# A mixture-of-experts block on one core: the last sequence's attention and shared experts move behind the routed tiles, and tokens are put in order in steps over two sequences

## The chip, the cores and the metric

The kernel runs on one core of a Trainium2 chip. The metric is the device time of one execution in microseconds (us). TensorE is called PE below, VectorE is DVE, ScalarE is ACT, GpSimd is POOL and SyncE is SP.

## The reference

There are 16 sequences of 512 tokens with 256 features. With `xn = layernorm(x)`, the output is `x + attention(xn) + ffn(xn)`, all in float32:

```
q, k = elu(xn@Wq+bq)+1, elu(xn@Wk+bk)+1 ;  v = xn@Wv+bv          # 16 heads of 16
attention = ((q @ (k^T v)) / max(q . sum(k), 1e-6)) @ Wo + bo    # linear, not causal, per sequence
shared    = swiglu(xn @ w_in^T) @ w_out^T                        # hidden 512
h         = swiglu(xn @ w1^T)                                    # hidden 512
group     = argmax of 2 group logits ; 2 best of its 4 experts, with weights p
routed    = sum over the 2 chosen experts e of  p_e * h @ w2[e]^T
```

A token therefore has one of 12 pairs of experts (6 in each group).

## The kernel before

**Dense part.** A loop over the 16 sequences `b` runs, for each: `front(b+1)` one sequence ahead (keys and logits into `pk`, queries into `pq`, the feature map, the routing in `route`), `summarize` (`pxk`, keys times inputs), `hidden_rows` (`phr`, the routed experts' hidden rows `h`, four tiles of 128 tokens, stored to a DRAM table `h_d`), `key_sum` and `attend` (`pks`, then normalized queries written to DRAM and read back turned), `hidden` (`phs`, the shared experts' hidden features `hs_all`), `mix` (`pvk`, DVE's `vk`, then `pm`, then ACT's copy `kvo`), and `gather` (`po`, for each of four token tiles four products with `wout_sb` and two with `kvo`, added to `res` by DVE and stored to `h_d` beside `h`). So one row of `h_d` holds 512 hidden values, 256 values of everything but the routed part, and two weights.

**Order.** Once all tokens are routed, `order` sorts them by pair. It counts (`pc`), computes each token's slot, and builds for eight groups `g` of eight token tiles the one-hot factors `lo` and `hi` on DVE, whose products `pi` on PE give, for each of 75 tiles of 128 slots, which token sits where. It is called at the start of the last sequence (`b = 15`), between `front` and `summarize`.

**Routed part.** Pairs of tiles (`class Tiles`): `rows` gathers 128 rows of `h_d` by an indirect DMA of POOL into one of four buffers that the dense part no longer uses; `turn` transposes the hidden values (12 ACT copies to `hb`, 7 DVE transposes to `hT`); `sums` multiplies with the pair's two experts (`py`), scales and adds the row's other 256 values on DVE (`y`), and scatters whole rows to `out` by an indirect DMA of POOL. 67 tiles are always run; more stand in a conditional block (`rest`, with `tc.If(n > i)`), which is skipped with these inputs. The first three pairs are gathered twice: before `gather(15)`, to turn the hidden values early, and after it, when the rest of the row has been stored.

**What sets the order.** Each engine runs its own instructions in the order in which the program lists them. A scheduler makes that list when the kernel is built; `tc.keep_in_program_order` pins an instruction in it, and `tc.issue_after(x)` keeps one behind another. An instruction that waits holds up all that is behind it on its engine. PSUM has six buffers named `mm` in a ring (all products but `po`, `py`'s included) and two named `py` (used by `po` and `pi`).

Lines that are spoken of below, with the numbers of the profile: L242 the DVE transpose that places `xnT` and `qT`, L424 `phr`, L443 `phs`, L482 `pvk`, L489 and L494 `vk`, L499 `pm`, L534 `po`, L535 its addition, L545 and L546 `pc`, L598 to L612 `lo` and `hi`, L614 `pi`, L654 `rows`, L673 to L686 `turn`, L703 `py`, L711 and L714 `y`, L717 the scatter, L783 the load of the count `n` into registers, L801 the conditional.

Of the kernel before, what the change touches and what calls it, by code (L numbers as in the profile page):

```python
# [15 lines left out]
P = 128  # L16
# [5 lines left out]
def block_kernel(  # L22
# [60 lines left out]
    wp = ctx.enter_context(tc.tile_pool(name="weights", bufs=1))  # L83
    xp = ctx.enter_context(tc.tile_pool(name="x", bufs=2))
    keep = ctx.enter_context(tc.tile_pool(name="keep", bufs=1))
# [11 lines left out]
    out_rows = out.rearrange("b s d -> (b s) d")  # L97

    def load_x(b, pieces=1):
        xt = xp.tile([P, NT, D], FP, tag="x", name=f"x_{b}")  # L100
        n = NT // pieces
        for i in range(pieces):
            nc.sync.dma_start(
                out=xt[:, ts(i, n), :], in_=x[b, ts(i, n * P), :].rearrange("(t p) d -> p t d", p=P)
            )
        return xt
# [109 lines left out]
    for c in range(NP):  # L216
        nc.gpsimd.memset(steps[:, c : c + 1], float(spots[c] - (spots[c - 1] if c else 0)))

    kk_all, qq_all, xn_all = (keep.tile([P, 2, NT, D], FP, name=f"{n}_all") for n in ("kk", "qq", "xn"))
    hs_all = keep.tile([P, KH, S], FP, name="hs_all")

# [192 lines left out]

    def hidden_rows(b, xnT):

        for t in range(NT):
            halves = []  # L420
            for half in range(2):
                ph = ps_mm.tile([P, HID], FP, tag="mm", name=f"phr_{b}_{t}_{half}")
                for k in range(KD):
                    nc.tensor.matmul(  # L424
                        ph, lhsT=xnT[:, k, ts(t, P)], rhs=w1_sb[:, k, ts(half, HID)],
                        start=(k == 0), stop=(k == KD - 1),
                    )
                halves.append(ph)
            sa = work.tile([P, HID], FP, tag="sa", name=f"sa_hr_{b}_{t}")
            nc.scalar.activation(sa, halves[0], AF.Silu)  # L430
            hr = work.tile([P, HID], FP, tag="hr", name=f"hr_{b}_{t}", bufs=3)
            nc.vector.tensor_tensor(hr, halves[1], sa, ALU.mult)  # L432
            nc.sync.dma_start(out=h_d[ts(b * NT + t, P), 0:HID], in_=hr)

    def hidden(b, xnT):

        h = hs_all
        for f in range(KH):
            halves = []
            for half in range(2):  # L440
                ph = ps_mm.tile([P, S], FP, tag="mm", name=f"phs_{b}_{f}_{half}")
                for k in range(KD):
                    nc.tensor.matmul(  # L443
                        ph, lhsT=win_sb[:, k, ts(half * KH + f, P)], rhs=xnT[:, k, :],
                        start=(k == 0), stop=(k == KD - 1),
                    )
                halves.append(ph)
            sa = work.tile([P, S], FP, tag="sa", name=f"sa_hs_{b}_{f}")
            nc.scalar.activation(sa, halves[0], AF.Silu)  # L449
            nc.vector.tensor_tensor(h[:, f, :], halves[1], sa, ALU.mult)  # L450
        return h

# [72 lines left out]

    def gather(b, res, qT, kvo, hs):

        taken = []
        for t in range(NT):
            po = ps_y.tile([P, D], FP, tag="py", name=f"po_{b}_{t}")  # L530
            parts = [(hs[:, f, ts(t, P)], wout_sb[:, f, :]) for f in range(KH)]
            parts += [(qT[:, c, ts(t, P)], kvo[:, c, :]) for c in range(KD)]
            for i, (a, w) in enumerate(parts):
                nc.tensor.matmul(po, lhsT=a, rhs=w, start=(i == 0), stop=(i == len(parts) - 1))  # L534
            taken.append(nc.vector.tensor_tensor(res[:, t, 0:D], po, res[:, t, 0:D], ALU.add))  # L535
            nc.sync.dma_start(out=h_d[ts(b * NT + t, P), HID:ROW], in_=res[:, t, :])
        return taken

    def order():
# [4 lines left out]
        pc = ps_mm.tile([P, 2 * NP], FP, tag="mm", name="pc")  # L544
        nc.tensor.matmul(pc[:, 0:NP], lhsT=before, rhs=total, start=True, stop=True)  # L545
        nc.tensor.matmul(pc[:, NP:], lhsT=ones, rhs=total, start=True, stop=True)  # L546
# [43 lines left out]
        where = keep.tile([P, TR], I32)  # L590
        nc.vector.tensor_copy(where, of)


        pi = ps_y.tile([P, 2 * TILES], FP, tag="py", name="pi")
        for g in range(TT // TG):
            row_of, tile_of = (place_of[:, i, ts(g, TG)].unsqueeze(2) for i in range(2))
            lo = xp.tile([P, TG, P], BF, tag="x", name=f"lo_{g}")
            nc.vector.tensor_tensor(  # L598
# [7 lines left out]
            )  # L606
            hi = work.tile([P, TG, 2, TILES], BF, tag="blocks", name=f"hi_{g}")
            nc.vector.tensor_tensor(
                hi[:, :, 0, :], at_tile,
                number[:, ts(g, TG)].unsqueeze(2).to_broadcast([P, TG, TILES]), ALU.mult,  # L610
            )
            nc.vector.tensor_scalar(hi[:, :, 1, :], at_tile, row, None, ALU.mult)  # L612
            for t in range(TG):
                nc.tensor.matmul(  # L614
                    pi, lhsT=lo[:, t, :], rhs=hi[:, t].rearrange("p i n -> p (i n)"),
                    start=(g + t == 0), stop=(g * TG + t == TT - 1),
                )
        pis = keep.tile([P, 2, TILES], FP)
# [15 lines left out]
        nc.vector.scalar_tensor_tensor(goal, tok, float(-P), free, ALU.add, ALU.add)  # L634
        return source, goal, where, filled

    regs = []

    rows_of = [a.rearrange("p a b c -> p (a b c)") for a in (kk_all, qq_all, xn_all)]
    rows_of.append(hs_all.rearrange("p a b -> p (a b)"))  # L640

    class Tiles:
# [16 lines left out]

        def turn(self, after=None):  # L660

# [3 lines left out]

            n, W = self.n, HID // NQ
            self.hT = work.tile([P, KH, 2 * P], FP, tag="xnT", name=f"hT_{self.tiles[0]}")
            to = self.hT.rearrange("p c (n a j) -> p n c a j", n=2, a=NQ)[:, 0:n]
            near = 1
            there = work.tile([P, NQ - near, 2, W], FP, tag="blocks", name=f"hb_{self.tiles[0]}")  # L670
            for a in range(near, NQ):
                for q in range(NQ):
                    nc.scalar.copy(  # L673
                        there[ts(q, Q), a - near, 0:n, :], self.hg[ts(a, Q), 0:n, ts(q, W)]
                    )
            wait = (lambda: tc.issue_after(after.ins)) if after else nullcontext
            for a in range(near):
                for q in range(NQ):
                    with wait():
                        nc.vector.transpose(  # L680
# [3 lines left out]
            for a in range(near, NQ):  # L684
                with wait():
                    self.turned = nc.vector.transpose(  # L686
                        to[:, :, :, a, :],
                        there[:, a - near, 0:n, :].rearrange("p n (c i) -> p n c i", i=Q),
                    )
            return self  # L690

        def sums(self, after=None):

            for j, i in enumerate(self.tiles):
# [14 lines left out]
                y = work.tile([P, D], FP, tag="y", name=f"y_{i}", bufs=4)  # L709
                with tc.issue_after(after.ins) if after else nullcontext():  # L710
                    nc.vector.scalar_tensor_tensor(  # L711
                        y, py[:, 0, :], base[:, D : D + 1], base[:, 0:D], ALU.mult, ALU.add
                    )
                nc.vector.scalar_tensor_tensor(  # L714
# [25 lines left out]
    for b in range(B):  # L740
        xn, xnT, _ = normed.pop(b)
        res, qq, kk = fronts.pop(b)
        if b + 1 < B:
            fronts[b + 1] = front(b + 1, normed[b + 1][1])
        else:

            nc.sync.dma_start(
                out=h_d[ts(b, S), HID:ROW].rearrange("(t p) h -> p t h", p=P), in_=res
            )
            *lists, filled = order()  # L750
            tiles = [Tiles(list(range(i, min(i + 2, SURE))), *lists) for i in range(0, SURE, 2)]
# [6 lines left out]
        if b + 3 < B:  # L758
            xs[b + 3] = load_x(b + 3)
        hidden_rows(b, xnT)  # L760
        ksb, (qT, turned) = sums, queries.pop(b)
        turned()
        if b + 1 < B:
            sums = key_sum(b + 1, fronts[b + 1][2])
            queries[b + 1] = attend(b + 1, fronts[b + 1][1], sums)
        hs = hidden(b, xnT)
        kvo = mix(b, xk, ksb)
        if b + 2 < B:
            normed[b + 2][2]()
        if b + 1 == B:  # L770
            for w in tiles[:AHEAD]:
                w.rows()
        taken = gather(b, res, qT, kvo, hs)
        if b + 1 == B:

            tiles[0].turn(taken[-2])
            for w in tiles[1:AHEAD]:
                w.turn(taken[-1])

# [7 lines left out]

    tiles[AHEAD].rows()
    for w in tiles[:AHEAD]:
        w.rows()  # L790
    for g, w in enumerate(tiles):
        if 0 < g < len(tiles) - AHEAD:
            tiles[g + AHEAD].rows()
        if 0 < g < len(tiles) - AHEAD + 1:
            tiles[g + AHEAD - 1].turn()

        w.sums(tiles[AHEAD - 1].turned if g == 0 else None)

# [12 lines left out]

    rest(SURE)


# [30 lines left out]
```

## Time and profile before

| what | value |
|---|---|
| three runs | 1079.85, 1085.42, 1088.38 us; median 1085.42 us |
| the profiled execution's own time | 1076.49 us |
| its span in the profile | 1074.8 us |
| PE busy | 1052.6 us (98%), 3404 matmuls |
| DVE busy | 661.1 us (62%) |
| ACT busy | 375.9 us (35%) |
| POOL busy | 244.9 us (23%) |
| DMA | 116.02 MB, mean 108 GB/s |

The profile is of one execution. "Busy" is the share of the span in which an engine had an instruction running; a matmul's end is modelled, so a busy PE is not a PE at its peak. A view "in order of time" gives the start, the length, the engine, the source line, the operation, the output and inputs, how many, and in brackets how long the engine had stood idle before and who released it.

### The profile page before, as it was taken

What the parts mean: (1) busy time and instruction counts of PE and PEld (TensorE: products, weight loads), DVE (VectorE), ACT (ScalarE), POOL (GpSimd) and SP (SyncE); (2) the same over time, 40 slices, a digit from 0 to 9 for tenths busy, and PEclk for the clock granted to TensorE, in tenths of its full rate; (3) what the DMA queues carried; (4) which work ended last, traced back from release to release, by engine and by line L of the source; (5) the groups of instructions that cost most, each with busy time, mean ns of one, the idle gap of its engine ahead of it and who ended that gap; (6) DMA issues with size and microseconds to landing.
All of it is one profiled execution on the core that took longest, in us unless ns stands there. A gap on an engine that the chain in (4) does not pass through costs nothing.

```text
span 1074.8 us, 11307 instructions
## 1 busy us (share of the span) xinstructions
PE 1052.6 (98%) x3404; PEld 624.7 (58%) x3404; DVE 661.1 (62%) x1744; ACT 375.9 (35%) x703; POOL 244.9 (23%) x313
## 2 busy tenths in 40 slices
PE   7999999999999999999999999999999999999996
PEld 6474848475756666575748484757566444444442
DVE  7947476565647474747465565646386576666663
ACT  3413132222222231313131322212113686667771
POOL 6102011020202020201011010202002665555552
PEclk9999999999999999999999999999999999999999
DMA  7243342424424242423231313131212654555440
GB/s 231 98 118 118 79 137 59 137 75 122 115 86 139 66 134 69 138 59 106 71 103 55 118 40 118 40 98 60 64 55 95 207 173 147 153 155 151 149 152 29
DMA packets 129054, 116.02 MB, mean 108 GB/s; under 512 B 72109, under 2 KB 113597, under 8 KB 128736
## 3 DMA queue, kind: packets, MB, share of 16 engines
q1 hardware_dynamic: 119120, 77.16, 24.0%
q0 software_dynamic: 9456, 37.59, 11.4%
q8 instruction: 29, 0.48, 0.2%
q10 hardware_dynamic: 416, 0.52, 0.1%
q14 instruction: 33, 0.27, 0.1%
HBM read 65.36 MB, written 50.27 MB: 108 GB/s over the span
## 4 chain that ended last, share of the span: by engine, by line
PE 91%; DVE 4%; DMA 2%; issue 1%; ACT 1%; POOL 1%; SPq 0%; POOLq 0%; ACTq 0%; DVEq 0%
PE phs L443 20%; PE py L703 20%; PE phr L424 19%; PE po L534 15%; PE pk L312 5%; PE pxk L469 5%; PE pq L323 5%; PE pm L499 1%; PE pvk L482 1%; DMA kk_all<-h_d,source 1%; PE pks L459 1%; ACT hb L673 1%; DMA xn_all<-h_d,source 0%; DMA x<-in_x 0%; DVE qm L300 0%
## 5 line engine op out<-in xcount | busy, mean ns | idle before, releaser
L703 PE MATMUL py<-w_sb,hT 128*128 x536 | 230.5, 592 | 2.0 <-DVE hT L686 2.0
L443 PE MATMUL phs<-xnT,win_sb 128*128 128x512 f32 x512 | 223.7, 593 | 0.0
L424 PE MATMUL phr<-w_sb,xnT 128*128 128x512 f32 x512 | 222.8, 592 | 0.0
L703 PEld LDWEIGHTS py<-w_sb,hT 128*128 128x128 f32 x536 | 101.7, 190 | 130.5 <-issue 129.3
L424 PEld LDWEIGHTS phr<-w_sb,xnT 128*128 128x128 f32 x512 | 97.1, 190 | 114.7 <-issue 105.9
L443 PEld LDWEIGHTS phs<-xnT,win_sb 128*128 128x128 f32 x512 | 96.6, 190 | 113.5 <-issue 110.0
L292 POOL TENSOR_TENSOR res<-x,bo_sb 128x1024 f32<-128x1024 f32 x16 | 38.9, 2432 | 435.0 <-DMA h_d<-res 324.0
L534 PE MATMUL po<-wout_sb,hs_all 128*128 128x256 f32 x512 | 123.6, 379 | 0.0
L535 DVE TENSOR_TENSOR res<-po,res 128x256 f32<-128x256 f32 x64 | 27.2, 424 | 131.8 <-PE po L534 131.8
L534 PEld LDWEIGHTS po<-wout_sb,hs_all 128*128 128x128 f32 x512 | 96.1, 190 | 12.4
L450 DVE TENSOR_TENSOR hs_all<-phs,sa_hs 128x512 f32<-128x512 f32 x64 | 43.4, 679 | 90.2 <-PE phs L443 84.9
L449 ACT ACTIVATE sa_hs<-phs 128x512 f32<-128x512 f32 x64 | 38.2, 597 | 157.8 <-PE phs L443 152.4
L717 POOL DMA_INDIRECT out<-y,goal x67 | 67.7, 1010 | 76.2 <-DVE y L714 65.5
L301 ACT ACTIVATE km<-km 128x1024 f32<-128x1024 f32 x16 | 16.9, 1058 | 178.0 <-DVE km L300 172.9
L432 DVE TENSOR_TENSOR hr<-phr,sa_hr 128x512 f32<-128x512 f32 x64 | 43.7, 684 | 55.0 <-PE phr L424 32.1
L430 ACT ACTIVATE sa_hr<-phr 128x512 f32<-128x512 f32 x64 | 38.0, 597 | 99.0 <-PE phr L424 93.1
L534 PE MATMUL po<-kvo,qT 128*128 128x256 f32 x256 | 67.0, 384 | 0.0
L312 PE MATMUL pk<-wkr_sb,xnT 128*128 128x266 f32 x256 | 61.0, 391 | 1.7 <-DVE xnT L242 1.7
L469 PE MATMUL pxk<-kk_all,xn_all 128*128 128x256 f32 x256 | 57.9, 379 | 0.0
L323 PE MATMUL pq<-wq_sb,xnT 128*128 128x256 f32 x256 | 57.8, 379 | 0.0
L456 POOL TENSOR_TENSOR k<-kk_all 128x512 f32<-128x512 f32 x16 | 27.6, 1723 | 125.4 <-DVE sm L358 119.3
L312 PEld LDWEIGHTS pk<-wkr_sb,xnT 128*128 128x128 f32 x256 | 48.9, 192 | 10.8 <-DVE xnT L242 2.1
(148 smaller groups left out, 1261.0 us busy)
## 6 DMA issues: line engine op xcount, KB each, us to landing
h_d<-hr SPq DMA_DIRECT2D x64, 256.0 KB, 2.6
h_d<-res SPq DMA_DIRECT2D x64, 129.0 KB, 2.0
q_d<-qq_all SPq DMA_DIRECT2D x16, 512.0 KB, 2.8
qb<-q_d SPq DMA_DIRECT2D x64, 128.0 KB, 2.6
w_sb<-in_w SPq DMA_DIRECT2D x64, 128.0 KB, 3.5
x<-in_x SPq DMA_DIRECT2D x15, 512.0 KB, 4.3
xn_d<-xn_all SPq DMA_DIRECT2D x14, 512.0 KB, 3.0
xb<-xn_d SPq DMA_DIRECT2D x56, 128.0 KB, 3.2
```

The source lines that it names most:

```text
L292: nc.gpsimd.tensor_tensor(res[:, :, 0:D], xs.pop(b), bo_sb.unsqueeze(1).to_broadcast([P, NT, D]), ALU.add)
L312: nc.tensor.matmul(pk, lhsT=xnT[:, k, ts(t, P)], rhs=wkr_sb[:, k, :], start=(k == 0), stop=(k == KD - 1),)
L323: nc.tensor.matmul(pq[:, t, :], lhsT=xnT[:, k, ts(t2 + t, P)], rhs=wq_sb[:, k, :], start=(k == 0), stop=(k == KD - 1),)
L424: nc.tensor.matmul(ph, lhsT=xnT[:, k, ts(t, P)], rhs=w1_sb[:, k, ts(half, HID)], start=(k == 0), stop=(k == KD - 1),)
L432: nc.vector.tensor_tensor(hr, halves[1], sa, ALU.mult)
L443: nc.tensor.matmul(ph, lhsT=win_sb[:, k, ts(half * KH + f, P)], rhs=xnT[:, k, :], start=(k == 0), stop=(k == KD - 1),)
L449: nc.scalar.activation(sa, halves[0], AF.Silu)
L450: nc.vector.tensor_tensor(h[:, f, :], halves[1], sa, ALU.mult)
L469: nc.tensor.matmul(pxk[:, c, :], lhsT=xn[:, t, ts(c, P)], rhs=kk[:, t, :], start=(t == 0), stop=(t == NT - 1),)
L534: nc.tensor.matmul(po, lhsT=a, rhs=w, start=(i == 0), stop=(i == len(parts) - 1))
L703: nc.tensor.matmul(py.rearrange("p j d -> p (j d)"), lhsT=self.hT[:, f, ts(j, P)], rhs=w2_sb[:, f, bass.ds(regs[i % TR], 2 * D)], start=(f ...
L717: stored = nc.gpsimd.indirect_dma_start(out=out_rows, out_offset=bass.IndirectOffsetOnAxis(ap=self.goal[:, i : i + 1], axis=0), in_=y, in_ ...
```

## The change

Five things change together.

1. For the last sequence no `gather` is done. Its `res` (input plus output bias) and its two weights are stored to `h_d` already at `b = 14`, so the routed tiles add only these. After all routed tiles, behind the conditional block, two DMAs (one of SP, one of ACT) read the last sequence's rows of `out` back into `far`; the four `po` products are made there, DVE adds them to `far`, and four plain DMAs write the rows again.
2. `order` becomes a generator. `hidden_rows`, `gather` and two places between them call its next step: the count and the slots while `phr(14)` runs, `lo` and `hi` of the groups from `b = 14`'s `attend` on, the products `pi` between the `po` of 14 and the `phr` of 15. The `pi` and the first `pc` are pinned in PE's order. For that, `x` gets a lasting tile `x_all`, in which `lo` lies; `hi` lies in parts of `qq_all`, `kk_all` and `xn_all`.
3. At `b = 15`, `hidden_rows` comes first, then the end of `order`, then `summarize`; the first three pairs' `rows` are issued before `hidden(15)`, and two of them are turned behind its second quarter (`made`). The second gather of these pairs is gone, and the four row buffers are now `qq_all, x_all, kk_all, xn_all` (before: `kk_all, qq_all, xn_all, hs_all`), since `hs_all` is kept to the end.
4. In `gather(b)` for all `b` up to 13, the additions of token tiles 2 and 3 are now kept behind the transpose that places `xnT(b+2)`. In the built program this moves one instruction: at `b = 0` the transpose stands ahead of two of the four additions and no longer behind all four.
5. The `po` of the last two sequences use the ring `mm`.

In the built program, on PE, the order around `mix` differs too: before, `pm(14)` stood behind three products of `po` and `pm(15)` likewise; after, `pm` follows directly on `pvk` in both sequences.

```diff
-            taken.append(nc.vector.tensor_tensor(res[:, t, 0:D], po, res[:, t, 0:D], ALU.add))
+            with tc.issue_after(placed.ins) if placed and t > 1 else nullcontext():
+                nc.vector.tensor_tensor(res[:, t, 0:D], po, res[:, t, 0:D], ALU.add)
             nc.sync.dma_start(out=h_d[ts(b * NT + t, P), HID:ROW], in_=res[:, t, :])
+            between(b, then(t))
...
-        for g in range(TT // TG):
...
+        for g in range(TT // TG + 2):
+            if g > 1:
+                add(g - 2)
+                yield
+            if g < TT // TG:
+                marks(g)
+                yield
...
-    rows_of = [a.rearrange("p a b c -> p (a b c)") for a in (kk_all, qq_all, xn_all)]
-    rows_of.append(hs_all.rearrange("p a b -> p (a b)"))
+    rows_of = [a.rearrange("p a b c -> p (a b c)") for a in (qq_all, x_all, kk_all, xn_all)]
...
-        else:
+        if b + 2 == B:
             nc.sync.dma_start(
-                out=h_d[ts(b, S), HID:ROW].rearrange("(t p) h -> p t h", p=P), in_=res
-            )
-            *lists, filled = order()
+                out=h_d[ts(b + 1, S), HID:ROW].rearrange("(t p) h -> p t h", p=P), in_=fronts[b + 1][0]
+            )
+            steps_of_order = order()
+        if b + 1 == B:
+            hidden_rows(b, xnT, dict.fromkeys(range(NT), 2).get)
+            *lists, filled = next(steps_of_order)
...
+        if b + 1 < B:
+            hidden_rows(b, xnT, {2: 1}.get)
...
+        if b + 2 == B:
+            next(steps_of_order)
...
-        taken = gather(b, res, qT, kvo, hs)
+        if b + 1 < B:
+            gather(b, res, qT, kvo, hs, normed[b + 2][2]() if b + 2 < B else None, {0: 2, 1: 2, 3: 2}.get)
...
-    tiles[AHEAD].rows()
-    for w in tiles[:AHEAD]:
-        w.rows()
+    for i, w in enumerate(tiles[: AHEAD - 1]):
+        w.turn(made[2 * i + 1])
...
     rest(SURE)
+    for half, queue in enumerate((nc.sync, nc.scalar)):
+        far = work.tile([P, 2, D], FP, tag="hr", name=f"far_{half}", bufs=3)
+        queue.dma_start(
+            out=far, in_=out[B - 1, ts(half, 2 * P), :].rearrange("(t p) d -> p t d", p=P)
+        )
+        for j in range(2):
+            t = 2 * half + j
+            po = outputs(B - 1, t, qT, kvo, hs)
+            y = work.tile([P, D], FP, tag="y", name=f"last_{t}", bufs=4)
+            nc.vector.tensor_tensor(y, po, far[:, j], ALU.add)
+            (nc.sync, nc.scalar)[t % 2].dma_start(out=out[B - 1, ts(t, P), :], in_=y)
```

`outputs` holds the six products of one token tile that `gather` made before.

## The prediction

> **What bounds the kernel now.** I read the page's busy shares and chain first, then PE's idle gaps, then the DVE queue at the places that the change touches, then the end.
>
> ```profile
> PE 1052.6 (98%) x3404; PEld 624.7 (58%) x3404; DVE 661.1 (62%) x1744; ACT 375.9 (35%) x703; POOL 244.9 (23%) x313
> PE 91%; DVE 4%; DMA 2%; issue 1%; ACT 1%; POOL 1%; SPq 0%; POOLq 0%; ACTq 0%; DVEq 0%
> ```
>
> PE holds the span. The change takes no product away (`po`, `pi`, `pc` are moved), so it can win only where PE stands still: 22 us of 1074.8, of which some 8 lie before 40 us (loads, untouched) and 10.3 behind the last product. The timeline of PE has three gaps that the change reaches:
>
> ```profile
> 72.36 2.96 PE L312 MATMUL pk<-wkr_sb,xnT 128*128 128x266 f32 x12 [1.67 <-DVE xnT L242]
> ...
> 832.61 27.73 PE L703 MATMUL py<-w_sb,hT 128*128 x64 [0.75 <-DVE hT L686]
> 861.64 4.53 PE L703 MATMUL py<-w_sb,hT 128*128 x10 [1.29 <-DVE hT L686]
> ```
>
> The first: PE waits at 72 us for a transpose that stood behind four additions. The others: routed tiles not yet turned when PE got to them. From 861.64 us on the 472 products run without a pause. The DVE queue at the first gap:
>
> ```profile
> 68.15 0.42 DVE L535 TENSOR_TENSOR res<-po,res 128x256 f32<-128x256 f32 x1 [2.16 <-PE po L534]
> 70.74 0.42 DVE L535 TENSOR_TENSOR res<-po,res 128x256 f32<-128x256 f32 x1 [2.17 <-PE po L534]
> 71.08 1.23 DVE L242 STREAM_TRANSPOSE xnT<-xb 128x1024 f32<-128x1024 f32 x1
> ```
>
> DVE idles 2.16 us twice for `po` while the transpose, whose data had landed by 62 us, waits behind. Next, how `pm` is covered in the chain at `b = 14`, and the chain's end:
>
> ```profile
> 770.89 0.89 PE pvk L482 x8
> 771.78 1.30 PE po L534 x6
> 773.08 0.99 PE pm L499 x4
> ...
> 1064.46 0.02 issue
> 1064.48 0.49 DVE y L711
> 1064.98 0.02 issue
> 1065.00 0.50 DVE y L714
> 1065.50 0.03 issue
> 1065.53 0.51 POOLq L783
> 1066.04 0.70 POOL out L717
> ```
>
> `pm` needs DVE's `vk`, and three `po` products (1.30 us) fill that wait. At the end, PE's last product is done at 1064.46; the sequencers' own records in the trace (no view prints them) give the rest: POOL issues the last scatter at 1065.76, sees it landed at 1068.9, settles its DMA semaphores until 1070.16, then a POOL drain lasts 3.75 us to 1073.93 and the closing barrier 0.8. Total behind PE: 1074.77 - 1064.46 = 10.3 us.
>
> [...] So the read-back waits for the last scatter; the trace prices that at 1065.76 to 1068.9, plus the settling. [...] after gaps of 1.7 us the clock stays full, and it halves 5.0 us after the last product. [...] Here DVE needs 0.52 us from the end of its branch to its next record; PE takes its branch 7 us early, hidden.
>
> **The change part by part.**
>
> *Transpose at b = 0* (edit 4). Placed behind two additions, it starts near 66 us; `pk` then follows `po` at once. The next product would have started at 70.53 (last start 70.32 plus a spacing of 0.216) and started at 72.36: gain **1.83**. PE has no gap from 80 to 780 us, so I let it stand; bounds 0 and 1.83.
>
> *The two gaps at the routed tiles* (edit 3). By start-to-start times they cost 0.91 and 1.46. After: last `pi`, then 1.83 us to the first gather (818.64 to 820.47 before), about 4.5 us landing, 12 ACT copies at 0.415, three transposes. The gather also needs `hr`'s last store (2.6 us), which makes some 2.3 us to its start instead. Walking the PE queue, that tile is turned 15 us behind the last `pi`, and `py` is reached at 21 us (`pxk` 3.5, `phs` 13.7, `pvk`, `pm` and a wait). The second pair is turned about 5 us before it is needed. Gain **2.37**, and 0.28 for one wait of PE before `pi` at 808. The six repeated gathers save POOL 6 us, beside PE: nothing.
>
> *Order over two sequences* (edit 2). `total` is there at 748.8, `pc` now comes at 753.3: no wait. But its DVE work is now ahead of `vk(14)`. DVE queue from `pcs` (754.0), in the built order, with before's durations: count and slots 0.18 + 4.55 (784.94 to 789.49 before), a `hr` 0.60, slot and places 0.77, `ksb` 0.38, `attend` 4.25 (1.22 + 1.22 + 0.13 + 0.47 + 1.21), `lo` 3 x 1.14, `at_tile` 2 x 0.69, `hi` 0.98 + 0.69, four `hs_all` 2.40, `vk` 0.64 + 0.42. Sum 20.66, so 774.68, and `pm` 0.2 later at 774.88. PE: `pc` to 753.63, then `phr` 3.43, `pks` 0.43, `phs` 13.73, `pvk` 0.89: 772.11. With `pm` right behind `pvk`, PE stands **2.77** us. Bounds 1.3 (`pvk` to `pm` with an idle DVE, as the chain shows) and 4. From there the marks lead PE: groups 1 and 2 are marked at 774.9 and 777.8, their `pi` come at 781 and 787; the last group is ready near 797, its `pi` comes at 804.
>
> *`pm(15)`* also follows `pvk` at once. Ahead of `vk` on DVE are the last `hs_all` (0.60) and one transpose (0.43), between its two steps another: 0.7 us later than the bare 1.3, less overlaps: cost **1.8**, bounds 1.3 and 3.
>
> *The end* (edits 1 and 5). `po(15)`, 48 records at 0.2155 = 10.35 us, goes from before the routed tiles to behind them. It can't start when the last `py` ends: PE waits for a DVE count that DVE raises only behind its last `y` and its branch, 1.78 us later in before's records (1064.45 to 1066.22). So `po` ends at 1.78 + 0.15 + 10.35 + 0.17 = 12.45 behind the last `py`. Then the last addition 0.45, a store 2.05, eight of SP's waits at 0.06, drain and barrier 0.95: 16.4 in all, of which 10.35 is moved work, leaving 6.05 against 10.3. The read-back lies beside `po`: scatter landed at 4.4, settled at 5.65, load issued at 6, landed at 9 to 10.3 (loads of `x`: 3.8 to 4.3 us median), while the last addition waits for PE until 12.45; POOL's 3.75 us drain runs there too. If the read-back took over 6.4 us, it would set the end. Gain **4.25**, bounds 2 and 5.
>
> *At nothing:* the row buffers and `x_all` change names, not distances; `po` in the ring `mm` finds free buffers.
>
> **Sum.** 1.83 + 2.37 + 0.28 - 2.77 - 1.8 + 4.25 = 4.2 us. The profiled execution took 1076.49 us (span 1074.8), so 1072.3. The three runs have a median of 1085.42, 8.9 above the profiled one, by nothing that the profile shows; I carry the difference over: **1081.2 us**.
>
> **Rivals.**
> (a) *DVE's queue costs more*: the order's steps before `vk(14)` and the transposes before `vk(15)` run at their upper ends, 4 and 3 us. For it: both `pm` have lost their cover. Against: the durations are measured, and DVE has slack behind. Then 2.4 less gain: 1083.6.
> (b) *The read-back sets the end*: the two loads are not done beside `po`, because of settling or slow landing (the longest landings in the page are 10.6 and 12.2 us, of 1 MB weights). At 9.5 us it costs 3: 1084.2. Against: the queues are almost empty by then.
> (c) *Slower*: [...] Place: DVE's queue ahead of `vk(14)`. If it is 2 us longer than summed, PE stands 4.8 us, the clock halves[...] Against: 2.77 is short of it, and 1.67 halved nothing.
>
> **How the numbers follow.** Forecast 0.64, (a) 0.18, (b) 0.11, (c) 0.07. The worst bounds together (0 + 2.37 - 4 - 3 + 2) give 2.6 us slower, the best (1.83 + 2.65 - 1.3 - 1.3 + 5) 6.9 faster. The three runs lie 8.5 us apart, so a median can be off by 4 or so. Range 1074 to 1087.5. A measurement of this kernel tells about 1% (10.9 us) from no change; no case reaches that either way: the three gaps (4.5 with the small wait) and the best end (5) make 9.5 even with no new pause. Spread between runs leaves 0.06 for faster and 0.03 for slower.
>
> **What would show it.** Right: no gap before `pk` at 70.5; no gap before the first `py`; gaps of 2 to 3.5 us before `pm(14)` and 1.3 to 2.5 before `pm(15)`; the last `py` near 1054, a PE gap of about 2 us before `po`, which ends near 1067, and a span near 1070.6. Wrong: gaps in the routed stage, the clock under 1.00 in any of these stretches, DVE's last addition waiting for `far` and not for `po`, or POOL's drain ending last.

## The result and the profile after

| | before | after |
|---|---|---|
| median | 1083.08 us (19 runs) | 1075.79 us (19 runs) |
| lowest and highest | 1076.86, 1088.38 | 1070.61, 1078.87 |
| profiled execution, span | 1076.49, 1074.8 | 1071.43, 1069.6 |

The ratio of after to before is 0.9926, with a 95% interval of 0.9908 to 0.9943: 8.0 us less, between 6.2 and 10. From profile to profile it is 5.06 us. The medians lie 7.3 us apart. So the change is faster by 0.7%, inside the range and within the 1% that the forecast took for what a measurement can tell.

The page of after, busy shares and the chain that ended last:

```profile
PE 1052.6 (98%) x3404; PEld 626.0 (59%) x3404; DVE 658.6 (62%) x1744; ACT 375.7 (35%) x703; POOL 239.0 (22%) x307
...
PE 1%; DVE 0%; issue 0%
PE po L547 1%; DVE last L868 0%
```

PE is busy for the same 1052.6 us as before, with the same 3404 products: what was won was idle time. The chain can be followed only back to the `po` at the end, because what releases those is a branch of DVE. POOL has six instructions less, the second gathers.

The timeline of PE, the places where before had its gaps and where new ones were expected:

```profile
70.69 3.76 PE L314 MATMUL pk<-wkr_sb,xnT 128*128 128x266 f32 x16
...
769.42 1.05 PE L494 MATMUL pvk<-xk,wv_sb 128*128 128x128 f32 x8
772.29 1.10 PE L511 MATMUL pm<-wo_sb,vk 128*128 128x256 f32 x4 [1.82 <-DVE vk L506]
...
821.88 1.13 PE L511 MATMUL pm<-wo_sb,vk 128*128 128x256 f32 x4 [1.71 <-DVE vk L506]
823.24 230.27 PE L747 MATMUL py<-w_sb,hT 128*128 x536 [0.22 <-ACT hb L718]
1055.45 1.97 PE L547 MATMUL po<-wout_sb,hs_all 128*128 128x256 f32 x8 [1.94 <-DVEq L845]
```

`pk` has no bracket: it follows `po` at once. All 536 `py` stand in one group, 230.27 us without a pause. Each `pm` has a pause of its own. The last one, 1.94 us before `po`, waits for DVE's queue, as foreseen. By start-to-start times less the usual spacing the four pauses are 1.99, 1.88, 0.38 and 2.11 us. For the third, the one before `py`, the line names ACT's `hb`; but ACT had ended the first pair's copies at 816.96, and DVE had turned that pair by 817.45, so the tile was ready, and what this product waits for stays open.

DVE at `b = 0`, where the transpose (L244) now stands ahead of two additions, and DVE at the end:

```profile
65.71 0.42 DVE L556 TENSOR_TENSOR res<-po,res 128x256 f32<-128x256 f32 x1 [1.67 <-PE po L547]
66.24 1.25 DVE L244 STREAM_TRANSPOSE xnT<-xb 128x1024 f32<-128x1024 f32 x1
68.30 0.42 DVE L556 TENSOR_TENSOR res<-po,res 128x256 f32<-128x256 f32 x1 [0.81 <-PE po L547]
...
1061.80 0.76 DVE L868 TENSOR_TENSOR last<-po,far 128x256 f32<-128x256 f32 x2 [7.25 <-DMA far<-out]
1063.49 0.42 DVE L868 TENSOR_TENSOR last<-po,far 128x256 f32<-128x256 f32 x1 [0.94 <-PE po L547]
1066.09 0.43 DVE L868 TENSOR_TENSOR last<-po,far 128x256 f32<-128x256 f32 x1 [2.17 <-PE po L547]
```

The first of DVE's final additions waits for the read-back, the last two for `po`. So the read-back, landed 8.2 us behind the end of the last `py` (1053.5 to 1061.7), is covered by the products.

### The profile page after: what moved, and what is told of

Read it like the earlier page. It is cut to its first block, busy times and chain, and to the rows that moved or that the text cites. A ratio compares the mean times of both kernels' runs of the same rounds, so it can differ in the third digit from the quotient of the medians.

```text
span 1069.6 us, 11317 instructions
## 1 busy us (share of the span) xinstructions
PE 1052.6 (98%) x3404; PEld 626.0 (59%) x3404; DVE 658.6 (62%) x1744; ACT 375.7 (35%) x703; POOL 239.0 (22%) x307
## 3 DMA queue, kind: packets, MB, share of 16 engines
q10 hardware_dynamic: 976, 1.05, 0.3%
## 5 line engine op out<-in xcount | busy, mean ns | idle before, releaser
L294 POOL TENSOR_TENSOR res<-x_all,bo_sb 128x1024 f32<-128x1024 f32 x16 | 38.8, 2428 | 435.3 <-DMA h_d<-res 324.0
```

Of the source, the lines that this page charges most:

```text
L294: nc.gpsimd.tensor_tensor(res[:, :, 0:D], xs.pop(b), bo_sb.unsqueeze(1).to_broadcast([P, NT, D]), ALU.add)
```

## The experiments

The twelve runs (ten changed kernels, and before itself profiled twice more) were made in four groups, each group on a chip of its own beside the kernel before. Ratios are to those runs of before. The kernel after was not among them: where it is compared with a variant, its numbers are those of the result, and the comparison goes through the two ratios to before.

### The transpose alone, and everything but the transpose

Before with edit 4 alone:

```diff
-            taken.append(nc.vector.tensor_tensor(res[:, t, 0:D], po, res[:, t, 0:D], ALU.add))
+            with tc.issue_after(placed.ins) if placed and t > 1 else nullcontext():
+                taken.append(nc.vector.tensor_tensor(res[:, t, 0:D], po, res[:, t, 0:D], ALU.add))
...
-        if b + 2 < B:
-            normed[b + 2][2]()
+        placed = normed[b + 2][2]() if b + 2 < B else None
```

> The kernel before with edit 4 alone: the additions of token tiles 2 and 3 stay behind the transpose that places xnT(b+2). My theory: the 1.67 us gap of PE before pk near 72 us goes, everything behind moves up by 1.8 us, span 1074.8 - 1.8 = 1073.0, ratio to before 0.998. Rival A (the gap's time is lost again to a later wait on a DMA): the gap goes, but a new one appears before 200 us and the span is 1074.8, ratio 1.000. Rival B [...]: ratio near 0.995, with the granted clocks of the timed runs higher than those of before.

After without edit 4:

```diff
-            with tc.issue_after(placed.ins) if placed and t > 1 else nullcontext():
-                nc.vector.tensor_tensor(res[:, t, 0:D], po, res[:, t, 0:D], ALU.add)
+            nc.vector.tensor_tensor(res[:, t, 0:D], po, res[:, t, 0:D], ALU.add)
```

> The changed kernel without edit 4 (the transpose at b = 0 stands behind all four additions again). My theory: a gap of 1.7 us before pk near 72 us returns and nothing else changes; 1.8 us slower than the changed kernel: span 1071.4, ratio to before 0.9945 if the changed kernel's is 0.9926. Rival A: no difference to the changed kernel, 0.9926. [...]

Measured: after without the edit has its gap back (below), and a span of 1070.8 us against 1069.6; ratio 0.9936 (0.9907 to 0.9965). In before with the edit alone the gap is gone (`pk` has no bracket), but the ratio is 0.9993 (0.9975 to 1.0012). Timeline of PE, first of after without the edit:

```profile
71.78 3.86 PE L314 MATMUL pk<-wkr_sb,xnT 128*128 128x266 f32 x16 [1.67 <-DVE xnT L244]
```

Then of before with the edit alone, at the same place and at the routed tiles:

```profile
70.60 3.76 PE L312 MATMUL pk<-wkr_sb,xnT 128*128 128x266 f32 x16
...
864.13 11.40 PE L704 MATMUL py<-w_sb,hT 128*128 x21 [5.61 <-DVE hT L687]
```

The edit is worth its 1.8 us at that gap in the trace. The timed runs of before neither show nor exclude it: the interval holds both 1.000 and the 0.998 that 1.8 us would make. Something larger varies there: this execution waits 5.61 us for the fifth pair's `hT`, where the profile that the forecast used has 1.29 us at the same place.

### The end: the last `po` ahead of the routed tiles

The `po` of the last sequence go back in front; DVE copies them into `hs_all`, and only the read-back, the addition and the store stay at the end.

```diff
+        if b + 1 == B:
+            for t in range(NT):
+                po = outputs(b, t, qT, kvo, hs)
+                nc.vector.tensor_copy(
+                    hs[:, 0:2, ts(t, P)], po.rearrange("p (f i) -> p f i", i=P)
+                )
...
-            po = outputs(B - 1, t, qT, kvo, hs)
...
-            nc.vector.tensor_tensor(y, po, far[:, j], ALU.add)
+            nc.vector.tensor_tensor(
+                y.rearrange("p (f i) -> p f i", i=P), hs[:, 0:2, ts(t, P)],
+                far[:, j].rearrange("p (f i) -> p f i", i=P), ALU.add,
+            )
```

> The changed kernel with the last sequence's po products made right behind mix(15), ahead of the routed tiles, and copied by DVE into free parts of hs_all; at the end DVE adds these to the rows read back. So the read-back and the second store stay, but no PE work lies beside them. My theory: the last py ends 10.4 us later than in the changed kernel (near 1063.9), the read-back lands 8.2 us behind it, four additions and the store follow, and the end lies 13.5 to 14 us behind the last py: span 1077.5, some 8 us more than the changed kernel's 1069.6, ratio to before 1.002. Rival (the read-back is cheap, and the gain at the end comes from the routed stage starting earlier): span within 2 us of the changed kernel's.

Measured: span 1077.5 us, ratio 0.9978 (0.9963 to 0.9993). DVE at the end:

```profile
1065.48 0.48 DVE L757 SCALAR_TENSOR_TENSOR y<-py,x_all,y 128x256 f32<-128x256 f32 x1
1072.92 1.43 DVE L873 TENSOR_TENSOR last<-hs_all,far 128x256 f32<-128x256 f32 x4 [6.96 <-DMA far<-out]
```

Without products beside it the read-back is bare: DVE's additions wait 6.96 us for it. The span ends 12.6 us behind the last `py` (1064.9), against 16.1 us in after, of which 10.35 are moved products: 5.75 us net. So `po` hides 6.9 us of this end, and that is what makes the end pay: without it the 12.6 us would be more than the 10.3 of before.

### The two pauses before `pm`

Four variants of after. (1) Both pauses covered: at `b = 14` the four shared products of `po_0` (eight records) stand between `pvk` and `pm`, at `b = 15` the last quarter of `phs` does. For that `mix` is cut in two, `mix` up to `vk` and `mixed` from `pm` on. (2) Only `b = 14` covered. (3) `lo` and `at_tile` of the first two groups kept behind `masked[0]`, the second step of `vk(14)`, on DVE. (4) The first group's `lo` made four times.

```diff
-        hs, made = hidden(b, xnT)
-        kvo = mix(b, xk, ksb)
+        if b + 1 == B and COVER15:
+            hs, made, vk = hidden(b, xnT, lambda: mix(b, xk, ksb))
+            kvo = mixed(b, vk)
+        else:
+            hs, made, _ = hidden(b, xnT)
+            vk = mix(b, xk, ksb)
+            if b + 2 == B and COVER14:
+                begun = outputs(b, 0, qT, None, hs, split=True)
+            kvo = mixed(b, vk)
```

> The changed kernel with both pm products covered again: at b = 14 the four shared products of po of token tile 0 stand between pvk and pm, at b = 15 pvk stands ahead of the last quarter of phs. My theory: the gaps of 1.82 and 1.71 us before pm go (at b = 14 perhaps 0.2 us is left, since DVE's vk comes 1.98 us behind pvk and the cover is 1.73), everything behind moves up 3.5 us, span 1066.1, ratio to before 0.989 to 0.990. Rival (PE's time is not the bound there; the tiles or the marks are then late): the gaps turn up before py or pi, span 1068 to 1070.

> The changed kernel with only pm(14) covered: the four shared products of po_0 stand between pvk and pm at b = 14; pm(15) still follows pvk. Of the 3.7 us that both covers gave in the profile this should give 1.9 to 2.0, a span near 1067.7 and a median 2 us under the changed kernel's, with 1.88 us left before pm(15). If the two pauses are not independent (the second one longer or shorter when the first is gone), the pause before pm(15) differs from 1.88 by over 0.3.

```diff
-            nc.vector.tensor_tensor(
-                lo, count.unsqueeze(1).to_broadcast([P, TG, P]), row_of.to_broadcast([P, TG, P]),
-                ALU.is_equal,
-            )
+            with tc.issue_after(masked[0].ins):
+                nc.vector.tensor_tensor(
+                    lo, count.unsqueeze(1).to_broadcast([P, TG, P]), row_of.to_broadcast([P, TG, P]),
+                    ALU.is_equal,
+                )
...
-        if b + 2 == B:
-            next(steps_of_order)
...
         if b + 2 == B:
             next(steps_of_order)
+            next(steps_of_order)
```

> The changed kernel with the first two groups' lo and at_tile kept behind vk(14) on DVE, so that some 4.8 us less work stands ahead of vk(14). If DVE's queue sets the pause before pm(14), it falls from 1.99 us to the chain's own latency, about 1.1 to 1.3 us (pvk's end to pm with an idle DVE), so 0.7 to 0.9 us less in the span, near 1068.8. If the latency of the chain is nearly all of it, under 0.3 us. The products pi of groups 0 and 1 come later on DVE and may make PE wait near 776 to 780 for up to 2 us, which would take the gain back: then the pause has only moved.

```diff
+            for _ in range(3 if g == 0 else 0):
+                nc.vector.tensor_tensor(
+                    lo, count.unsqueeze(1).to_broadcast([P, TG, P]), row_of.to_broadcast([P, TG, P]),
+                    ALU.is_equal,
+                )
```

> The changed kernel with the first group's comparison lo made four times and not once, 3 x 1.14 us more on DVE ahead of vk(14) with the same values. Theory (DVE's queue sets the pause before pm(14)): the pause grows from 1.99 us by 3.4 to 5.4 us. [...] Rival: a pause of this length leaves the clock full: 3.4 us up and a span of 1073. Rival (the pause is the fixed latency of the chain pvk, vk, pm): no growth.

The pauses are by start-to-start times; (1) and (2) have six timed runs each, (3) 15 and (4) nine.

| kernel | pause 14, pause 15 | span | median | ratio |
|---|---|---|---|---|
| after | 1.99, 1.88 | 1069.6 | 1075.79 | 0.9926 (0.9908 to 0.9943) |
| (1) both covered | 0.17, 0 | 1064.8 | 1067.2 | 0.9867 (0.9836 to 0.9899) |
| (2) b = 14 covered | 0.16, 1.87 | 1067.6 | 1069.7 | 0.9903 (0.9872 to 0.9934) |
| (3) marks behind | 1.32, 1.87 | 1073.4 | 1075.15 | 0.9925 (0.9907 to 0.9943) |
| (4) more on DVE | 3.53, 1.88 | 1076.0 | 1075.35 | 0.9935 (0.991 to 0.9961) |

The timeline of PE with both covered:

```profile
768.72 1.05 PE L498 MATMUL pvk<-xk,wv_sb 128*128 128x128 f32 x8
769.61 1.89 PE L561 MATMUL po<-wout_sb,hs_all 128*128 128x256 f32 x8
771.51 1.13 PE L519 MATMUL pm<-wo_sb,vk 128*128 128x256 f32 x4
...
814.17 3.60 PE L457 MATMUL phs<-xnT,win_sb 128*128 128x512 f32 x8
817.61 1.03 PE L519 MATMUL pm<-wo_sb,vk 128*128 128x256 f32 x4
818.47 16.90 PE L768 MATMUL py<-w_sb,hT 128*128 x39
```

No bracket is left here, the `py` pause included; the 2.11 us before the last `po` stay. This version beats before, and by its span and its ratio after too, though it was not run beside after. The pauses are independent: covering one leaves the other at 1.87.

With the marks behind `vk`, and with more work on DVE ahead of it:

```profile
774.01 1.13 PE L512 MATMUL pm<-wo_sb,vk 128*128 128x256 f32 x4 [1.16 <-DVE vk L507]
...
777.96 0.69 PE L651 MATMUL pi<-qq_all,x_all 128*128 128x150 bf16 x8 [0.22 <-DVE qq_all L647]
```

```profile
778.69 1.10 PE L511 MATMUL pm<-wo_sb,vk 128*128 128x256 f32 x4 [3.37 <-DVE vk L506]
```

So the pause is 1.32 us of bare latency from `pvk` over `vk` to `pm` (in (3) DVE stands idle before `vk`), and the rest is DVE's queue, one to one: in (4) the scheduler also moved a later `lo` and a step of `hi` behind `vk`, so that the queue from `pcs` to the end of `vk` took 21.44 us and not 19.9, 1.54 more, and the pause grew by 1.54. The expectation of 5.4 us had overlooked that move. The pause of 3.53 us didn't halve the clock: the eight `po` behind it took 1.89 us, as in after. In (3) part of the gain comes back at once: the first `pi` waits 0.39 us for its marks. The spans of (3) and (4) also hold pauses of 2.28 and 3.29 us near 19 us, at the first loads, which no edit touched and which after's profile doesn't have, and a granted clock of 0.998 where after has 1.000. In (3) this is seen at the first `py`: 19 of them take 10.09 us, 1.7 us more than after's first 19 (8.39). For (4) the same 1.7 us is taken as an estimate. With these the spans come out: 1069.6 - 0.67 + 0.39 + 2.28 + 1.7 = 1073.3 (measured 1073.4), and 1069.6 + 1.54 + 3.29 + 1.7 = 1076.1 (1076.0).

### The routed tiles: what varies in before

Before with a fifth buffer for rows (`x_all`), so that the fifth pair's gather doesn't wait for the first pair's additions:

```diff
     rows_of.append(hs_all.rearrange("p a b -> p (a b)"))
+    rows_of.append(x_all.rearrange("p a b c -> p (a b c)"))
...
     for w in tiles[:AHEAD]:
         w.rows()
+    tiles[AHEAD + 1].rows()
     for g, w in enumerate(tiles):
-        if 0 < g < len(tiles) - AHEAD:
-            tiles[g + AHEAD].rows()
+        if 0 < g < len(tiles) - AHEAD - 1:
+            tiles[g + AHEAD + 1].rows()
```

> The kernel before with a fifth buffer for gathered rows (x_all), so that the fifth pair's rows are issued right behind the repeated gathers and no longer behind the first pair's additions; everything else stays, the second gather too. Theory (the term for the gaps at the routed tiles was mis-sized, because the fifth pair has no slack there and is late by 1.5 us in one execution and by 5.8 in another): the gap in the products near 860 us goes (1.46 us in the profiled execution), and the timed median falls by more than that, 2 to 5 us against the kernel before on the same chip. Rival (the gap is always about 1.5 us and the timed gain beyond the forecast comes from somewhere else): a fall of 1 to 1.7 us, no more. Rival (not this wait at all, but the repeated gathers): the gap stays. The gap of 0.9 us before the first py stays in every theory.

Measured: 1086.54 us median, ratio 1.003 (1.001 to 1.005). The gap stayed, as the last rival had it; that the kernel got slower no theory had. This execution also has a pause of 3.8 us near 19 us with slow products behind it (five `pk` in 2.56 us, where before's first profile has sixteen in 3.77). Timeline, PE, then DVE, then ACT:

```profile
871.51 3.87 PE L707 MATMUL py<-w_sb,hT 128*128 x5 [5.53 <-DVE hT L690]
```

```profile
867.55 0.48 DVE L715 SCALAR_TENSOR_TENSOR y<-py,xn_all 128x256 f32<-128x256 f32 x1 [10.49 <-remote]
```

```profile
858.08 4.98 ACT L677 COPY hb<-x_all 32x256 f32<-32x256 f32 x12 [5.11 <-DMA x_all<-h_d,source]
```

The fifth pair's rows came early and ACT had copied them by 863.1, but DVE's transposes stood behind an addition `y` that DVE began only at 867.55. So neither buffer nor rows held PE up. That `y` needed the fifth tile's products, which PE had done near 855.7. The profile names `remote` as what released it.

Before without the second gather, before profiled again, and after with the second gather put back:

```diff
     tiles[AHEAD].rows()
-    for w in tiles[:AHEAD]:
-        w.rows()
```

> The kernel before without the second gather of the first three pairs: their rows keep the last 258 columns as the first gather found them, so the six tiles add values of the last sequence that are not final; nothing else is changed. Theory (the routed stage's late fifth pair, and PE's count reaching DVE late in the dense run of gathers, is what holds the typical execution of before some 7 us above its profiled one): without six gathers in a row DVE's first additions come 2 to 3 us sooner, the fifth pair's rows some 5 us sooner, the gap near 860 us goes, and the median falls by 4 to 8 us, with most clocks at 0.996 or 0.997. Rival (a gap of 1.5 us is all there is): a fall of 1 to 1.7 us and the same spread of clocks as before. Rival (the late fifth pair has another cause, such as its buffer or ACT's copies): the gap stays.

> The kernel before, profiled once more, to see an execution nearer to its median than the profiled one. Theory: a time of 1080 to 1085 us, a mean clock near 0.994, and near 860 us a gap in py of 4 to 7 us with a stretch at half clock behind it, as in the run with the early transpose alone. Rival: the time is above the first profile's by several us, but the gap near 860 us is again about 1.5 us and the rest lies elsewhere, for example at the loads before 30 us.

```diff
             tiles[g + AHEAD - 1].turn()
+        if g == 0:
+            for v in tiles[:AHEAD]:
+                v.rows()
```

> The changed kernel with the second gather of the first three pairs put back, of the same rows, behind the fourth pair's rows: six more gathers in a row at the start of the routed tiles. Theory (this run of gathers is what hurts in before): DVE's first additions wait for it, a later pair's hT is late, PE has a gap of 1 to 6 us in py between 840 and 870 us, and the median rises by 3 to 8 us. Rival (in the changed kernel the pairs are far enough ahead, so that the gathers are hidden, and only the early start of the rows matters): no gap, and a median within 1 us of the changed kernel's.

All three ran on a chip on which before is quicker: 1077.72 us median, and only 3 of its 43 runs had a clock at or under 0.994, against 20 of 45 and 24 of 40 in the first two groups (medians 1082.19 and 1082.93). Without the second gather: 1075.83 us, ratio 0.9988 (0.9974 to 1.0002), and in the timeline of PE no gap behind the first `py`:

```profile
836.84 38.46 PE L703 MATMUL py<-w_sb,hT 128*128 x89 [0.75 <-DVE hT L686]
```

The second profile of before: 1081.03 us, a gap in PE's starts of 1.95 us in `py`; its extra time lies near 19 us (a pause of 2.98 us with slow products behind it, six `pk` in 2.74 us). After with the second gather: 1076.94 us, ratio 0.9972 (0.9956 to 0.9988), and no gap:

```profile
829.82 45.65 PE L747 MATMUL py<-w_sb,hT 128*128 x106
```

So the second gather makes the gap in before (its removal takes it away), but it makes none where the pairs are further ahead. Here the rivals were right: in the one profile of before on this chip the gap is under 2 us, and its removal gained 1.3 us (at most 2.8), not 4 to 8.

Before profiled a third time, on a fourth chip:

> The kernel before profiled a third time, since the second profile (1081.03 us) showed a gap of only 1.95 us near 860 us and its extra time before 30 us. Theory (in most executions behind the result PE's count reaches DVE late in the run of gathers): if the time is 1081 us or more and the mean clock is at or under 0.994, the trace has a gap of 4 to 7 us in py near 860 us, DVE idle for over 4 us without a wait that the profile names, and a stretch of about 7 us at half clock behind it. Rival (the extra time is that of the first loads): a gap of 2.3 to 4 us near 19 us with a half-clock stretch of 3.4 us or more behind it, and only 1.5 to 2 us near 860 us. If the run is a quick one (under 1079 us), neither is to be seen and the point stays as it is.

Measured: 1081.38 us, clock 0.994, and the gap and the half clock that the theory had asked for. PE, then DVE, in order of time:

```profile
832.29 27.73 PE L703 MATMUL py<-w_sb,hT 128*128 x64 [0.74 <-DVE hT L686]
863.97 11.31 PE L703 MATMUL py<-w_sb,hT 128*128 x20 [3.94 <-DVE hT L686]
```

```profile
850.60 0.48 DVE L714 SCALAR_TENSOR_TENSOR y<-py,qq_all,y 128x256 f32<-128x256 f32 x1
858.02 0.48 DVE L711 SCALAR_TENSOR_TENSOR y<-py,xn_all 128x256 f32<-128x256 f32 x1 [6.93 <-PE py L703]
...
860.91 1.78 DVE L680 STREAM_TRANSPOSE hT<-kk_all 32x256 f32<-32x256 f32 x4 [1.89 <-PE py L703]
```

And busy time by stretches (PEclk, the granted clock, is the third column from the end):

```profile
core 0: us, PE busy (x) PEld busy (x) DVE busy (x) ACT busy (x) POOL busy (x), PEclk, DMA share, GB/s
850.00:857.00 7.00, 7.00 (x18) 3.17 (x17) 1.05 (x3) 1.44 (x4) 5.47 (x6) 1.00 0.68 198
857.00:864.00 7.00, 3.06 (x9) 1.06 (x7) 3.98 (x10) 6.74 (x18) 2.00 (x3) 0.87 0.49 148
864.00:871.00 7.00, 7.00 (x11) 3.06 (x12) 5.94 (x15) 2.12 (x6) 4.79 (x5) 0.64 0.39 106
```

DVE does 1.05 us of work in 7 us while PE runs at full rate, then PE stands 3.94 us and has 11 products in 7 us in place of 18. The granted clock of 0.87 and 0.64 makes some 6.9 us at half clock by estimate (0.13 and 0.36 of 7 us, twice), and all `py` together were busy for 2.5 us longer than in before's first profile (233.0 against 230.5). DVE is said to wait for PE's `py`, but the fifth tile's last product had ended at 849.6 (832.29 + 39 x 0.429 + 0.6). The trace's records of counts and of waits, which no view prints, tell more. The two other counts that this `y` waits for, those of its rows and of its buffer, had come by 850.71, where DVE's own record of waiting for them ends; only PE's was left. PE's count is recorded as raised at 842.87, next at 857.99, and at 860.89, 862.36 and 862.45, while a tile ends every 3.43 us; in before's first profile it is raised within 0.1 us of each tile's end (836.33, 839.76, 843.20 and so on). Some raises have no record (the fourth tile's, due at 846.3, although DVE's next transposes need that tile done and ran at 847.3), so the times at which DVE went on weigh more: 858.02 for the fifth tile, and 860.91 for transposes that needed the sixth, done at 853.2. So DVE went on 8.4 and 7.7 us behind the products, and PE's count reached it about 8 us late. Before with the early transpose and before with five buffers have the same pattern: the fifth tile's `y` begins 7.2 and 11.9 us behind its products, with three and four raises recorded 0.09 us apart, at 861.05 and 867.52.

What makes the count late stays open. It is in three of the five profiles of before and its variants that gather twice, and begins in stretches with a DMA share of 0.65 to 0.76. It is neither in the first two profiles of before, which gather alike (the first with shares of 0.65 and 0.91 there), nor in those of after and of after with the second gather. So the DMA share alone does not decide it.

## Why the prediction was right, and where it was not

**The direction, the bound and the places** were right: no product less, every gap and every missing gap where it was said to be, but for a wait of 0.38 us before the first `py`.

**Transpose**: 1.83 us forecast; its gap is gone in after, and back in after without the edit (1.83 us by starts, 1.2 us of span).

**Routed tiles**: the first pair was turned 15.4 us behind the last `pi` (15 forecast), and no `py` behind the first waits.

**`pm(14)`**: 2.77 forecast, 1.99 measured. PE's side of the sum held (18.1 us from `pcs` to the end of `pvk`, in both); DVE's queue was mis-sized, 20.66 us summed and 19.9 measured (752.25 to 772.15). That this queue sets the pause is shown by the runs that shorten and lengthen it.

**`pm(15)`**: 1.8 forecast, 1.88 measured.

**The end**: 16.4 us behind the last `py` forecast, 16.1 measured. That the read-back lies beside `po` is shown by the run with `po` ahead.

**The sum** for the profiled execution was 1072.3 us and came to 1071.43. The forecast for the timed runs, 1081.2 us, lay 5.4 above the 1075.79 measured, which is near the lower end of the range. Of this, 2.3 us are the three early runs, whose median (1085.42) was above that of nineteen (1083.08); 0.9 stand in the profiled execution; and 2.2 are a smaller distance of the median from the profiled execution in after (4.4 us) than in before (6.6).

**What was mis-sized** is the term for the two gaps at the routed tiles, 2.37 us, and with it the step that carries the 8.9 us between the median and the profiled execution over unchanged, "by nothing that the profile shows". The profile was of a quick execution. In the third profile of before the two gaps are 0.91 and 4.11 us and the slower products behind them cost another 2.5 (`py` busy for 233.0 us against 230.5): 7.5 us where 2.37 were counted, 5.1 more. That is shown for this execution.

How often it happens is not shown. Clocks at or under 0.994, as that execution had, came in about half of before's runs in the first two groups (44 of 85). If each of them had the late count, some 2.7 us are due to it on average, an estimate, and 4.2 + 2.7 = 6.9 lies within the 6.2 to 10 measured. But a clock of 0.994 in before says only that some 6.5 us of clock were missing (0.6% of 1080 us, an estimate), of which PE's idle tail makes 2.65 (in before's first profile the last 5.3 us were granted 0.50). The first loads can cost clock too: four of the profiles, of kernels of both kinds, have a PE pause of 2.28 to 3.8 us near 19 us, and in two of them the slow `pk` behind it are shown above. In the first group that is a weak rival: the 14 runs there of after without the edit and of both covered, which load alike, had clocks of 0.998 and over, where 20 of 45 of before had 0.994 or less. In the second group, where three of the four profiles have the pause at the loads, it stays open. The estimate also leaves out what the new pauses cost after in its slower executions. On the chip on which before rarely has such clocks, after with the second gather gained 0.28% or 3.0 us (1.3 to 4.7), no more than the forecast; after as it is was not run there.

**Rival (c)** had its place right and its point wrong: the pause before `pm(14)` was 1.99 us and not 4.8, and even 3.53 us there left the clock full. On the other hand `py` ran slower by 1.7 us in the run with the marks behind (10.09 us for the first 19 against 8.39), behind the pauses of 1.87 and 0.38 us at `pm(15)` and `py`; in after's own profile, with 1.88 and 0.38, the granted clock stayed at 1.00. What decides between the two was not shown. That such a loss comes in some executions and not in others fits after's median of 4.4 us above its profiled execution, to which the pause at the loads can add. It also fits the version with both pauses covered, whose six runs lie within 2.4 us; its trace is 4.8 us shorter than after's and its ratio to before 0.0059 lower (6.4 us), but the intervals of the two ratios are too wide to tell 6.4 from 4.8.

**Rivals (a) and (b)** fell: the pauses were shorter than forecast for 14 and nearly as forecast for 15, and `po`, not the read-back, set the end.

## What to carry to other kernels

One profiled execution shows one state of a tight place: where an engine waits 1 to 2 us for a long chain of gather, copies and transposes, look at the spread of the runs and at their clocks before pricing that wait, because the same wait can be several us longer in another execution (1.46 us in one profile of before, 4.11 in another). A PE pause near 2 us cost its length in after's profile (1.88 us) and, with the slower products behind it, 1.7 us more in the run with the marks behind; cover it with independent products (four of `po`, a quarter of `phs` were enough), before shaving the engine that it waits for. A transfer that must follow the last result can be hidden (6.9 us here) if work that doesn't depend on it is kept back for that moment.

## What the runs showed of the hardware

- *The granted clock.* In before's first profile it is 1.00 until 5.0 us after PE's last product (1064.5 to 1069.5) and 0.50 in the 5.3 us that follow. Behind a pause of 3.94 us (third profile of before) it averages 0.64 over 7 us, and behind one of 5.61 us (before with the early transpose) 0.68; each time PE has 11 products in the 7 us, where at 1.00 it has 17 or 18. Behind the 3.53 us before `pm(14)`, with more on DVE, the eight `po` took 1.89 us, as in after. Behind 1.87 and 0.38 us at `pm(15)` and `py`, with the marks behind, the first 19 `py` took 10.09 us; after, with 1.88 and 0.38, needed 8.39. So in these runs the length of one pause did not decide it. What does was not shown.
- *The late count.* In a dense run of gathers (six in 7 us on POOL) PE's count reached DVE 7 to 12 us late in three profiles (8.4, 7.2 and 11.9 us for the fifth tile), with raises recorded 0.09 us apart behind that. The cause is open. The views put DVE's wait down to "issue", "remote" or "PE py", each time with the products long done; such a bracket is to be held against the producer's own end.
